# A selective scan in units of 1024 columns: where the carry is copied, and when the halves of each sum are issued

## The chip, the core and the metric

The kernel runs on one core of a Trainium2 chip. The metric is the time of one execution on the device, in microseconds (us); the number compared is the median over runs. In the profile PE is TensorE (PEld its weight loads), DVE is VectorE, ACT is ScalarE, POOL is GpSimd, and SP is SyncE, which issues all of this kernel's DMAs.

## The reference

Two vision blocks follow each other on 8 images of 64x64 tokens with 192 channels. The first is a Mamba-2 block with a depthwise convolution, two scan directions and an MLP. The second splits the channels: 96 go through three convolutions, 96 through a selective scan. The change lies in the selective scan of the second block:

```python
# four directions k: rows, columns, and both reversed; 192 channels d, 16 states n, 4096 tokens l
def step(h, t):
    u_t, d_t, b_t, c_t = t
    h = jnp.exp(d_t[..., None] * A) * h + (d_t * u_t)[..., None] * b_t[:, :, None, :]
    return (h, jnp.einsum('bkdn,bkn->bkd', h, c_t))
...
_, ys = lax.scan(step, h0, scan_in)
ys = jnp.moveaxis(ys, 0, -1) + Ds[None, :, :, None] * xs4
```

So for each direction, channel and state there is a recurrence h[l] = a[l] h[l-1] + b[l] along the tokens, and each output is a sum over the 16 states of h[l] times C[l].

## The kernel before, in words

**Units.** The scan is cut into units. A unit is 128 partitions (8 channels x 16 states) by 1024 tokens (LC). 16 units make a tile of 128 channels, three tiles make a step (the channels of two directions), and each image takes 4 steps forward and 4 steps of the reversed directions: 8 images x 8 steps x 3 tiles x 16 = 3072 units. The unit with the same channels and the next 1024 tokens comes one step, 48 units, later; what it needs is the last column of h of this unit, its carry, kept in the tile `carry`, one column per unit of a step.

**What a unit does.** `fetch(q)` brings in the step sizes, repeated over the states, six units ahead (SP, tile dA, seven buffers). `decay(q)` takes their exponential on ACT two units ahead (L1450). `spread(q)` lets PE repeat the inputs over the states into PSUM, one unit ahead (L1458, tile dB, two buffers). `weigh(q)` multiplies dB by B on DVE (L1473). `scan(q)` runs the recurrence on DVE into h (L1480, seven buffers) and then has POOL multiply h in place by C (L1482), on all columns but the last, which the next step needs unmultiplied. One unit later `carry_on(q)` has ACT copy that column to `carry` (L1488) and then multiply it by C in place (L1489).

**Sums over states.** For four units together `gather` has PE sum the products over the states, with a matrix of zeros and ones: four units go to four groups of 32 partitions of one PSUM tile, 512 columns at a time (L1500, tile acc). After each half ACT copies the PSUM tile to y (L1505, two buffers of y). `store` writes y to DRAM in four DMAs (L1513).

**The order.** All instructions are pinned: each engine runs its own in the order of the program, and so do SP's DMA issues. The main loop goes over q. At the start of a unit come fetch(q+6), weigh(q), and, when due, the making of a gather and a store. Then come two halves. In each half one piece of the gather under way is issued (`next(gathering, None)`), then a piece of other work, then a piece of the preparation of the next tile. The first half ends with carry_on(q-1), spread(q+1) and scan(q), the second with decay(q+2). A gather for units q-5 to q-2 begins in the units q with (q - 2) % 4 == 3. Its first half's matmuls are issued in that unit's first half; the copy of them and the second half's matmuls in its second half; the second copy in the next unit's first half. The store comes at the start of the unit after.

**Work beside.** While the scan of one image runs, `beside` issues everything else: the first block of the next image (conv0, ssd, mlp0), the convolution branch, the scan's inputs, and sums and outputs of earlier images. It has a budget of PE time for each half unit, and a gather's half takes 1.6 us from it (`beside.spend`). All these pieces take their PSUM tiles from one pool of four banks (`cx.one`), the sums over states too.

Of the kernel before, what the change touches and what calls it, by code (L numbers as in the profile page):

```python
# [9 lines left out]
F32 = mybir.dt.float32  # L10
BF16 = mybir.dt.bfloat16
AF = mybir.ActivationFunctionType
# [5 lines left out]
L = HH * WW  # L18
# [20 lines left out]
LC = 1024  # L39
# [1272 lines left out]
def selective_scan(cx, us, ys, beside, images, start_image, tail):  # L1312
# [8 lines left out]
    nc, tc, pin, k = cx.nc, cx.tc, cx.pin, cx.k  # L1321
    AHEAD, BEHIND = 6, 2
    halves = [slice(q * 512, (q + 1) * 512) for q in range(LC // 512)]
    steps = []
# [6 lines left out]
    U = len(units)  # L1331
    per_image = U // images

    def order(ap, g):
        return reversed_free(ap) if g == 1 else ap
# [8 lines left out]
    with (  # L1344
# [6 lines left out]
        u_of, rows_of, bc_of, delta_of, du_of, carries = {}, {}, {}, {}, {}, {}  # L1351
        dAs, dBs, hs, late = {}, {}, {}, []

        def load(m, t):
            image, g, s = steps[m]
            u = wp.tile([128, LC], F32, tag=f"u{t}", name=f"u{t}")
            pin(nc.sync.dma_start(out=u, in_=us(image)[t][:, s * LC : (s + 1) * LC]))
            u_of.setdefault(m, []).append(u)

        def project(m):  # L1360

            image, g, s = steps[m]
            if s == (0, L // LC - 1)[g]:
                carries[image, g] = cp.tile([128, 3, UN], F32, tag="carry", name="carry")
                pin(nc.gpsimd.memset(carries[image, g], 0.0))
            rows = wp.tile([NXP, LC], F32, tag="rows", name="rows")
            for here in halves:
                ps = cx.one("ps_xp")
                for t in range(3):
                    pin(nc.tensor.matmul(  # L1370
                        ps[:NXP], lhsT=k["xp"][:, g, t, :], rhs=u_of[m][t][:, here], start=t == 0, stop=t == 2
                    ))
                    beside.spend(1.2)
                    yield
                pin(nc.scalar.copy(rows[:, here], ps[:NXP]))
            yield
            yield
            bcd = dp.tile([4 * NS, LC], F32, tag="bcd", name="bcd")
            pin(nc.sync.dma_start(out=bcd, in_=rows[0 : 4 * NS]))
            rows_of[m] = rows, bcd  # L1380

        def lay(m, e, i):

            t = wp.tile([128, LC], F32, tag=f"bc{i}{e}", name=f"bc{i}{e}")
            at = NS * (2 * i + e)
            pin(nc.sync.dma_start(out=t, in_=repeated(rows_of[m][1][at : at + NS], True)))
            bc_of.setdefault((m, e), []).append(t)
# [54 lines left out]
        def fetch(q):  # L1442
            n, i = units[q]
            dAs[q] = np_.tile([128, LC], F32, tag="dA", name="dA", bufs=AHEAD + 1)
            pin(nc.sync.dma_start(out=dAs[q], in_=repeated(delta_of[n][UD * i : UD * (i + 1)], False)))

        def decay(q):
            n, i = units[q]
            m, t = tiles[n]
            pin(nc.scalar.activation(dAs[q], dAs[q], AF.Exp, scale=k["neg_a"][:, steps[m][1], t, i : i + 1]))  # L1450

        def spread(q):

            n, i = units[q]
            dBs[q] = pw.tile([128, 2, 512], F32, tag="w", name="dB")
            for half in range(2):
                at = 32 * (2 * (i % 2) + half)
                pin(nc.tensor.matmul(  # L1458
                    dBs[q][:, half, :], lhsT=k["spread"][at : at + 3 * UD, :], rhs=du_of[n][at : at + 3 * UD, i // 2, :],
                    start=True, stop=True,  # L1460
                ))

        def of(q):

            n, i = units[q]
            m, t = tiles[n]
            image, g, _ = steps[m]
            return *bc_of[m, (i // 8 if t == 2 else t)], carries[image, g][:, t, i : i + 1], 0 if g == 1 else LC - 1, g

        def weigh(q):  # L1470

            dBs[q] = dBs[q].rearrange("p a b -> p (a b)")
            pin(nc.vector.tensor_mul(dBs[q], dBs[q], of(q)[0]))  # L1473

        def scan(q):

            _, C_, carry, last, g = of(q)
            dA, dB = dAs.pop(q), dBs.pop(q)
            h = hs[q] = np_.tile([128, LC], F32, tag="h", name="h", bufs=4 + BEHIND + 1)
            pin(nc.vector.tensor_tensor_scan(order(h, g), order(dA, g), order(dB, g), carry, ALU.mult, ALU.add))  # L1480
            rest = slice(1, LC) if last == 0 else slice(0, LC - 1)
            pin(nc.gpsimd.tensor_mul(h[:, rest], h[:, rest], C_[:, rest]))  # L1482

        def carry_on(q):

            _, C_, carry, last, _ = of(q)
            end = hs[q][:, last : last + 1]
            pin(nc.scalar.copy(carry, end))  # L1488
            pin(nc.scalar.activation(end, end, AF.Identity, scale=C_[:, last : last + 1]))  # L1489

        def gather(q):

            n, i = units[q]
            m, t = tiles[n]
            image, g, s = steps[m]
            y = np_.tile([128, LC], F32, tag="y", name="y")
            for here in halves:
                ps = cx.one("acc")
                for v in range(4):
                    pin(nc.tensor.matmul(  # L1500
                        ps[32 * v : 32 * (v + 1)], lhsT=k["gather"], rhs=hs[q - 3 + v][:, here], start=True, stop=True
                    ))
                beside.spend(1.6)
                yield
                pin(nc.scalar.copy(y[:, here], ps))  # L1505
            for v in range(4):
                del hs[q - 3 + v]
            late.append((ys(image)[g][t][UD * (i - 3) : UD * (i + 1), s * LC : (s + 1) * LC], y))

        def store():  # L1510
            rows, y = late.pop()
            for v in range(4):
                pin(nc.sync.dma_start(out=rows[UD * v : UD * (v + 1)], in_=y[32 * v : 32 * v + UD]))  # L1513
# [16 lines left out]
        for q in range(U + BEHIND):  # L1530
            n, at = divmod(q, UN)
            if q < U:
                m, t = tiles[n]
                if q == 0 or q == U - per_image + 2 * BEHIND:
                    start_image(q // per_image, 2 * (per_image - 24))
                if at == 0:
                    coming, due = prepare(n + 1) if n + 1 < len(tiles) else None, 0
                if at in (4, 5):
                    if t == 0:
                        lay(m, 1, at - 4)  # L1540
                    if t == 1 and m + 1 < len(steps):
                        lay(m + 1, 0, at - 4)
                if t == 2 and m + 1 < len(steps):
                    image = steps[m + 1][0]
                    new = image != steps[m][0]
                    if new and at == UN - 8:
                        beside.finish()
                    if UN - 8 <= at < UN - 5:
                        load(m + 1, at - UN + 8)
                    if new and at == UN - 6 and image + 1 < images:  # L1550
                        start_image(image, 2 * per_image)
                    if at == UN - 6:
                        following = project(m + 1)
                if q + AHEAD < U:
                    fetch(q + AHEAD)
                weigh(q)
            elif q == U:
                carry_on(q - 1)
            if (q - BEHIND) % 4 == 3 and q > BEHIND:
                gathering = gather(q - BEHIND)  # L1560
            if (q - BEHIND) % 4 == 1 and q > BEHIND + 1:
                store()
            if q < U:
                for half in range(2):
                    next(gathering, None)
                    beside.half()
                    if coming is not None and 2 * at + half == due:
                        due = next(coming, 2 * UN)
                    if following is not None and t == 2 and at >= UN - 5:
                        next(following, None)  # L1570
                    if half == 0:
                        if q > 0:
                            carry_on(q - 1)
                        if q + 1 < U:
                            spread(q + 1)
                        scan(q)
                    elif q + 2 < U:
                        decay(q + 2)
# [160 lines left out]
```

## Time and profile before

| what | value |
|---|---|
| median of 3 runs | 16,441.98 us (16,431.81 to 16,492.6) |
| span of the profiled execution | 16,436.7 us |
| granted TensorE clock, mean | 0.827 |
| DMA | 3241 MB, 197 GB/s, the hardware queue's packets take 78.5% of 16 engines' span |
| decay, L1450 | 3072 x 1144 ns on ACT |
| sum over states, L1500 | 12,288 passes, 617 ns each in the median |

The profiled execution is one run of its own, and its span goes from the first to the last instruction; it lies 5 us below the median of the runs. A group of instructions is told by line, engine and operation, what it writes and reads, how often it runs, its busy time and the mean of one; behind the second bar stands the time that the engine was idle just before it and what ended most of that. A wait is told as who waited, for whom, the total, how often, and the longest.

### The profile page before, as it was taken

What the parts mean: (1) busy time and instruction counts of PE and PEld (TensorE: products, weight loads), DVE (VectorE), ACT (ScalarE), POOL (GpSimd) and SP (SyncE); (2) the same over time, 40 slices, a digit from 0 to 9 for tenths busy, and PEclk for the clock granted to TensorE, in tenths of its full rate; (3) what the DMA queues carried; (4) which work ended last, traced back from release to release, by engine and by line L of the source; (5) the groups of instructions that cost most, each with busy time, mean ns of one, the idle gap of its engine ahead of it and who ended that gap; (6) DMA issues with size and microseconds to landing.
All of it is one profiled execution on the core that took longest, in us unless ns stands there. A gap on an engine that the chain in (4) does not pass through costs nothing.

```text
span 16436.7 us, 210821 instructions
## 1 busy us (share of the span) xinstructions
PE 13372.1 (81%) x69608; PEld 4636.5 (28%) x69608; DVE 12230.0 (74%) x9264; ACT 10412.7 (63%) x20023; POOL 10527.5 (64%) x5766
## 2 busy tenths in 40 slices
PE   8977887788877897878888788777898788878876
PEld 4423322332223321333223332233322333211111
DVE  2178887886878767887678876788767886778994
ACT  4466677665775757757576575766657666655654
POOL 3158766775668656686567765677656775566773
PEclk9987888789887897878888798887988779877766
DMA  3288888788887888878888778887778877888885
GB/s 89 84 218 195 210 205 225 190 204 208 204 219 187 205 205 207 209 191 204 208 208 207 198 196 198 217 205 197 204 193 221 198 202 205 193 227 200 211 204 137
DMA packets 1602582, 3241.31 MB, mean 197 GB/s; under 512 B 390152, under 2 KB 841368, under 8 KB 1601496
## 3 DMA queue, kind: packets, MB, share of 16 engines
q1 hardware_dynamic: 1601496, 3227.83, 78.5%
q8 instruction: 559, 9.16, 0.3%
q14 instruction: 527, 4.32, 0.1%
HBM read 2548.91 MB, written 678.18 MB: 196 GB/s over the span
## 4 chain that ended last, share of the span: by engine, by line
PE 30%; DMA 16%; DVE 14%; ACT 13%; POOL 7%; issue 5%; SPq 2%; DVEq 0%; ACTq 0%; POOLq 0%
DVE h L1480 9%; DMA dA<-dld 5%; PE acc L1500 5%; DVE dB L1473 4%; PE ps_c L895 4%; PE ps_cv L343 3%; POOL h L1482 3%; ACT dA L1450 3%; PE dB L1458 2%; DMA dus<-dud 2%; PE ps_sum L1193 1%; ACT L107 1%; PE ps_m L799 1%; PE ps_y L696 1%; ACT h L830 1%
## 5 line engine op out<-in xcount | busy, mean ns | idle before, releaser
L1482 POOL TENSOR_TENSOR h<-h,bc 128x1023 f32<-128x1023 f32 x3072 | 7228.8, 2354 | 4585.2 <-DVE h L1480 3895.8
L1480 DVE TENSOR_TENSOR_SCAN h<-dA,carry,dB 128x1024 f32<-128x1024 f32 x3072 | 7200.8, 2344 | 820.7 <-ACT dA L1450 257.6
L1473 DVE TENSOR_TENSOR dB<-dB,bc 128x1024 f32<-128x1024 f32 x3072 | 3736.3, 1216 | 1827.5 <-PE dB L1458 1823.9
L1450 ACT ACTIVATE dA<-dA,neg_a 128x1024 f32<-128x1024 f32 x3072 | 3512.9, 1144 | 29.3 <-DMA dA<-dld 24.1
L1500 PE MATMUL acc<-h,gather 128*32 128x512 f32 x12288 | 2364.1, 730 | 596.5 <-ACT h L1489 329.0
L1458 PE MATMUL dB<-dus,spread 24*128 24x512 bf16 x6144 | 1370.2, 435 | 664.5 <-DVE h L1480 620.1
L1505 ACT COPY y<-acc 128x512 f32<-128x512 f32 x1536 | 884.8, 576 | 750.3 <-PE acc L1500 677.4
L895 PE MATMUL ps_c<-p,conv_w 96*96 96x512 f32 x2304 | 1287.7, 685 | 37.9 <-ACT p L915 26.9
L1488 ACT COPY carry<-h 128x1 f32<-128x1 f32 x3072 | 584.2, 190 | 856.9 <-DVE h L1480 854.4
L1458 PEld LDWEIGHTS <-spread 24*128 24x128 bf16 x6144 | 308.0, 93 | 2837.2 <-issue 1395.5
L1489 ACT ACTIVATE h<-h,bc 128x1 f32<-128x1 f32 x3072 | 905.2, 295 | 143.3 <-ACT carry L1488 1.8
L696 PE MATMUL ps_y<-X,M 64*64 64x64 f32 x12288 | 605.6, 270 | 418.6 <-issue 232.7
L624 ACT ACTIVATE M<-ps_d,ln_dt 128x64 f32<-128x64 f32 x3072 | 669.1, 335 | 314.6 <-PE ps_d L630 304.6
L343 PE MATMUL ps_cv<-pad,diag 64*64 64x512 f32 x6912 | 841.0, 605 | 7.1 <-ACT y L1505 5.1
L1500 PEld LDWEIGHTS acc<-h,gather 128*32 128x32 f32 x12288 | 311.2, 117 | 1636.3 <-issue 1040.1
L107 ACT ACT_TABLE_LOAD x577 | 740.3, 1283 | 10.0
L696 PEld LDWEIGHTS ps_y<-X,M 64*64 64x64 f32 x12288 | 548.8, 180 | 606.5 <-issue 275.5
L629 PE MATMUL ps_d<-R,after 128*128 128x384 f32 x1024 | 606.4, 685 | 31.2 <-ACT bc L618 14.6
L895 PEld LDWEIGHTS ps_c<-p,conv_w 96*96 96x96 f32 x2304 | 372.6, 180 | 785.5 <-issue 725.4
L618 ACT COPY bc<-ps_t 64x256 f32<-64x256 f32 x256 | 93.4, 365 | 716.7 <-PE ps_t L613 716.5
L373 PE MATMUL ps_h<-oa,w1a 128*128 128x256 f32 x1536 | 484.0, 438 | 76.6 <-ACT y L1505 32.2
L1370 PE MATMUL ps_xp<-u,xp 128*108 128x512 f32 x768 | 470.0, 699 | 92.5 <-DMA u<-u 76.0
(243 smaller groups left out, 18412.4 us busy)
## 6 DMA issues: line engine op xcount, KB each, us to landing
dA<-dld SPq DMA_DIRECT2D x3072, 512.0 KB
dud<-terms SPq DMA_DIRECT2D x192, 768.0 KB
dus<-dud SPq DMA_DIRECT2D x2304, 64.0 KB
bc<-bcd SPq DMA_DIRECT2D x256, 512.0 KB
y<-yrows SPq DMA_DIRECT2D x256, 384.0 KB
u<-u SPq DMA_DIRECT2D x192, 512.0 KB
dld<-dl SPq DMA_DIRECT2D x192, 512.0 KB
y<-y SPq DMA_DIRECT2D x3072, 32.0 KB
```

The lines of the kernel that those rows point to most:

```text
L107: self.pin(self.nc.scalar.preload_act_table_set("natural_log_exp_and_others"))
L343: pin(nc.tensor.matmul(ps[64 * b : 64 * (b + 1)].rearrange("p (h w) -> p h w", w=WW), lhsT=diag[:, t, :], rhs=pad[64 * i : 64 * (i + 1), b ...
L696: pin(nc.tensor.matmul(psy[d][here, h * HP : (h + 1) * HP], lhsT=M[here, d, h, :], rhs=X[here, d, h, :], start=True, stop=True,))
L895: pin(nc.tensor.matmul(ps.rearrange("p (h w) -> p h w", w=WW), lhsT=w[:, t, :], rhs=pad[:, dy : dy + RB, dx : dx + WW], start=t == 0, stop ...
L1450: pin(nc.scalar.activation(dAs[q], dAs[q], AF.Exp, scale=k["neg_a"][:, steps[m][1], t, i : i + 1]))
L1458: pin(nc.tensor.matmul(dBs[q][:, half, :], lhsT=k["spread"][at : at + 3 * UD, :], rhs=du_of[n][at : at + 3 * UD, i // 2, :], start=True, s ...
L1473: pin(nc.vector.tensor_mul(dBs[q], dBs[q], of(q)[0]))
L1480: pin(nc.vector.tensor_tensor_scan(order(h, g), order(dA, g), order(dB, g), carry, ALU.mult, ALU.add))
L1482: pin(nc.gpsimd.tensor_mul(h[:, rest], h[:, rest], C_[:, rest]))
L1489: pin(nc.scalar.activation(end, end, AF.Identity, scale=C_[:, last : last + 1]))
L1500: pin(nc.tensor.matmul(ps[32 * v : 32 * (v + 1)], lhsT=k["gather"], rhs=hs[q - 3 + v][:, here], start=True, stop=True))
L1505: pin(nc.scalar.copy(y[:, here], ps))
```

## The change

The carry's copy moves from ACT to POOL, right behind the scan and ahead of POOL's product, which then goes over all 1024 columns in place. It is left out for the last step of an image and direction, whose carry nobody reads. ACT's two instructions of `carry_on` go. In `gather` three empty pieces (`yield`) are put ahead of the second half's matmuls, so that they are issued three half units later than before, in the first half of the unit after next, and the second copy in that unit's second half. The store moves by one unit. h has eight buffers instead of seven and y one instead of two.

```diff
 def of(q):
...
-            image, g, _ = steps[m]
-            return *bc_of[m, (i // 8 if t == 2 else t)], carries[image, g][:, t, i : i + 1], 0 if g == 1 else LC - 1, g
+            image, g, s = steps[m]
+            more = s != (L // LC - 1, 0)[g]
+            bc = bc_of[m, (i // 8 if t == 2 else t)]
+            return *bc, carries[image, g][:, t, i : i + 1], 0 if g == 1 else LC - 1, g, more
...
-            h = hs[q] = np_.tile([128, LC], F32, tag="h", name="h", bufs=4 + BEHIND + 1)
+            h = hs[q] = np_.tile([128, LC], F32, tag="h", name="h", bufs=4 + BEHIND + 2)
             pin(nc.vector.tensor_tensor_scan(order(h, g), order(dA, g), order(dB, g), carry, ALU.mult, ALU.add))
-            rest = slice(1, LC) if last == 0 else slice(0, LC - 1)
-            pin(nc.gpsimd.tensor_mul(h[:, rest], h[:, rest], C_[:, rest]))
-
-        def carry_on(q):
-
-            _, C_, carry, last, _ = of(q)
-            end = hs[q][:, last : last + 1]
-            pin(nc.scalar.copy(carry, end))
-            pin(nc.scalar.activation(end, end, AF.Identity, scale=C_[:, last : last + 1]))
+            if more:
+                pin(nc.gpsimd.tensor_copy(carry, h[:, last : last + 1]))
+            pin(nc.gpsimd.tensor_mul(h, h, C_))
...
-            y = np_.tile([128, LC], F32, tag="y", name="y")
+            y = np_.tile([128, LC], F32, tag="y", name="y", bufs=1)
             for here in halves:
+                if here is halves[1]:
+                    yield
+                    yield
+                    yield
                 ps = cx.one("acc")
...
-            elif q == U:
-                carry_on(q - 1)
             if (q - BEHIND) % 4 == 3 and q > BEHIND:
                 gathering = gather(q - BEHIND)
-            if (q - BEHIND) % 4 == 1 and q > BEHIND + 1:
+            if (q - BEHIND) % 4 == 2 and q > BEHIND + 2:
                 store()
...
                     if half == 0:
-                        if q > 0:
-                            carry_on(q - 1)
                         if q + 1 < U:
                             spread(q + 1)
                         scan(q)
```

More of the change, by code (lines that the diff above doesn't have):

```diff
@@ L1475, in scan @@
         def scan(q):
-            _, C_, carry, last, g = of(q)
+            _, C_, carry, last, g, more = of(q)
             dA, dB = dAs.pop(q), dBs.pop(q)
-            h = hs[q] = np_.tile([128, LC], F32, tag="h", name="h", bufs=4 + BEHIND + 1)
+            h = hs[q] = np_.tile([128, LC], F32, tag="h", name="h", bufs=4 + BEHIND + 2)
             pin(nc.vector.tensor_tensor_scan(order(h, g), order(dA, g), order(dB, g), carry, ALU.mult, ALU.add))
-            rest = slice(1, LC) if last == 0 else slice(0, LC - 1)
-            pin(nc.gpsimd.tensor_mul(h[:, rest], h[:, rest], C_[:, rest]))
-        def carry_on(q):
-            _, C_, carry, last, _ = of(q)
-            end = hs[q][:, last : last + 1]
-            pin(nc.scalar.copy(carry, end))
-            pin(nc.scalar.activation(end, end, AF.Identity, scale=C_[:, last : last + 1]))
+            if more:
+                pin(nc.gpsimd.tensor_copy(carry, h[:, last : last + 1]))
+            pin(nc.gpsimd.tensor_mul(h, h, C_))
         def gather(q):
```

## The prediction

> **What bounds the kernel now.** I read the page first: the busy times, then the chain that ended last.
>
> ```profile
> PE 13372.1 (81%) x69608; PEld 4636.5 (28%) x69608; DVE 12230.0 (74%) x9264; ACT 10412.7 (63%) x20023; POOL 10527.5 (64%) x5766
> PE 30%; DMA 16%; DVE 14%; ACT 13%; POOL 7%; issue 5%; SPq 2%; DVEq 0%; ACTq 0%; POOLq 0%
> ```
>
> No engine is full, and no engine holds more than a third of the chain. 3072 units in 15,290 us (first scan to last) make 4.98 us a unit. DVE needs 2344 + 1216 = 3560 ns of that for the scan and the product into dB; PE, with all that runs beside, needs about 4.3. The two hold each other through the two dB buffers: spread(q+1) waits for scan(q-1), weigh(q+1) waits for spread(q+1). So what counts is not who is busiest but who comes late at a hand-over. That is in the list of waits and in the costliest groups:
>
> ```profile
> L1482 POOL TENSOR_TENSOR h<-h,bc 128x1023 f32<-128x1023 f32 x3072 | 7228.8, 2354 | 4585.2 <-DVE h L1480 3895.8
> L1505 ACT COPY y<-acc 128x512 f32<-128x512 f32 x1536 | 884.8, 576 | 750.3 <-PE acc L1500 677.4
> L1488 ACT COPY carry<-h 128x1 f32<-128x1 f32 x3072 | 584.2, 190 | 856.9 <-DVE h L1480 854.4
> L1489 ACT ACTIVATE h<-h,bc 128x1 f32<-128x1 f32 x3072 | 905.2, 295 | 143.3 <-ACT carry L1488 1.8
> ```
>
> ```profile
> DVE dB L1473 <- PE dB L1458: 1823.9, 718, 99.4
> ...
> ACT carry L1488 <- DVE h L1480: 854.4, 526, 10.1
> ...
> PE acc L1500 <- ACT h L1489: 329.0, 96, 15.9
> PEld acc L1500 <- POOL h L1482: 307.3, 196, 5.4
> ...
> DVE h L1480 <- ACT dA L1450: 257.6, 77, 14.4
> ...
> DVE h L1480 <- ACT carry L1488: 231.4, 90, 9.9
> ```
>
> The columns are total us, times, longest. The reader is to see that ACT's two one-column instructions cost 1489 us of busy time and stop ACT, which works in order, for 854 us behind a scan, and that PE's sums over states stand 329 us for the second of them. The two last rows are one thing: in the records of those waits decay(q) ends 90 ns before the scan, and the carry of unit q-2 merely runs right behind it. So the scan stood 489 us, 167 times, for late decays.
>
> **The change, part by part.** The sum is made against the profiled span, 16,436.7 us; the median of the runs, 16,442, lies 5 above.
>
> (1) The sum over states no longer waits for ACT. It needed the later of POOL's product and ACT's last column; by the records ACT's column ends 0.7 us after the product in the median unit, 6.9 us after in one of ten. PE's waits inside the first halves that ended on h are 133, 368 us together. Were the product alone, 0.3 us later, to release them, 304 us would go. What arrives at the end? The sum stands in PE's order ahead of the next unit's spread, and DVE's idle time before weigh is 945 ns in the unit behind a sum's start against 478 on average in the other three: 0.467 x 768 = 359 us, which holds the wait and the sum's own matmuls. Bounds 0 and -304; I take half, **-150**.
>
> (2) Decays come earlier. Ahead of each decay ACT loses 190 + 295 ns and, per unit, 854/3072 = 0.28 us of standing: 0.76 us. 167 late decays x 0.76 = 127 if one unit's relief arrives; all 489 at most, 0 at least (table loads and activations of the side work are the rest of the lateness). I take **-130**. Other PSUM evictions gain too; not counted.
>
> (3) POOL gets 2304 copies of 128x1 (three of four steps hand a carry on). No such row exists. Nearest:
>
> ```profile
> L418 POOL COPY pad<-pad 128x132 f32<-128x132 f32 x72 | 20.9, 295 | 117.1 <-PE ps_cv L343 117.1
> ...
> L932 POOL COPY p<-p 96x64 f32<-96x64 f32 x56 | 13.2, 235 | 0.0
> ```
>
> ```profile
> L1365 POOL MEMSET carry<- x16: 127/144/153, 791.1 to 15387.1; 128x48 f32 x16
> ```
>
> From 132 to 64 columns the copy loses 60 ns, so at one column about 180; bounds 127 and 235. That is 415 us of POOL (290 to 540). POOL idles 3896 us waiting for scans, which hides most; without that cover all 415 would show. It shows where POOL is the path: 522 us of the chain are this product, 222 instructions, x 0.75 x 0.18 = 30; and beside the layer-0 state recurrence (646 units of 5.83 us by the records, POOL idle 20%) up to 646 x 0.135 = 87. I take **+50**. The product over 1024 columns instead of 1023 adds 2.3 ns x 3072 = 7 us of POOL, at nothing. The copy waits for the scan as the product did, with only the product and POOL's side work queued behind; the carry's reader comes 48 units later, so no scan waits.
>
> Product and scan share no time visibly: the product takes 2326 to 2390 ns and the scan 2325 to 2350 over all 3072, however they overlap, so the copy adds nothing to DVE.
>
> (4) One buffer of y. The first copy of the next sum (half 1 of unit Q+4) must now wait until the four stores of the last (issued at the start of Q+3) have landed. By the completions in the trace (a DMA's landing is the last update of its semaphore before that semaphore's next issue) the last of four stores lands 4.3 us after the first issue in the fastest twentieth, 6.1 in the median, over 10.1 in one of ten. Shifting each landing by one unit and comparing it with the copy's start as it is now: median 0.7 us to spare, but 43% lack time, 1099 us in all. With the issue as early as SP can (0.7 us behind the scan) it is 29% and 515 us. Behind the copy on ACT stand the evictions of the side work and decay(Q+6). What takes the sting out: the lacking cases lie where DVE is nearly full (four units take 18.0 us, DVE idle 1.8; in the others 21.3 and 4.5), a decay ends 4.6 us before its scan in the median, ACT is idle 37%, and (1) and (2) give ACT back 0.76 x 4 = 3.1 us per sum against 1.4 taken. Bounds 0 and +1099; I take a tenth, **+100**.
>
> [...]
>
> (5) Halves apart, eight buffers of h. The second half moves from half 1 of unit Q to the start of Q+2: eight of PE's passes (1.07 us at the full clock) and one 576 ns copy. PE does not wait there, its h being long done. scan(Q+3) takes a buffer read by it, but weigh(Q+3) already stands behind spread(Q+3), which PE issues after it: no new wait. Gain: half the sum's load leaves unit Q+1; at most what (1) leaves of 359, 209. Loss: weigh(Q+3) comes behind 1.07 us more PE work, at worst 768 x the same 0.467 = 359 again. I take **-40**.
>
> [...] The row: the granted clock is 0.827 on average, and a matmul of the sums takes 617 ns in the median but 730 on average. [...]
>
> (6) SP. The stores (four issues of 287 ns) keep their number and go behind the next unit's fetch, half a unit behind the second copy instead of a whole one. That distance is 2.8 us in the median now, so SP will often stand for ACT, 1 to 2 us, with later fetches and the side work's loads queued behind. A dA lands 16 us (5%: 6.4) before its decay starts: **0**; loads of the side work that are closer are in the range.
>
> Sum: -150 - 130 + 50 + 100 - 40 = -170; 16,267, so with the 5 us **16,270 us**.
>
> **Rivals.** *Y's single buffer becomes ACT's stop* (slower). Place: the copy at L1505, once per four units. Price: 1099 us of ACT. The gains without it are 270, 0.35 us per sum, so from the point where a quarter of those 1.43 us per sum reaches PE or DVE, it decides. For it: DMA engines are 80 to 90% busy in most slices and landings reach 10 us; PSUM has four single banks, so an ACT that stands soon stops PE. Against: the cover in (4). At 40%: 440 - 270 = +170, 16,610 us.
>
> *The waits change places* (no change). Freed from ACT, the sum waits for POOL (307 us on that row already, each 0.18 later), DVE still waits 1824 us for PE, whose work is the same. Only (2) remains, at 127, and pays for (3) and (4): 16,442 - 127 + 150 = 16,465 us. For it: PE holds the largest share of the chain.
>
> *ACT was the pacer more than its chain share says* (faster still). All of 304 + 489 goes, y costs nothing: 16,437 - 793 + 50 = 15,694, with the 5 us 15,700 us. Against: the page's chain holds ACT at 13% only.
>
> **How the numbers follow.** Forecast 0.42, larger gain 0.08, no change 0.20, slower by y 0.30. About 0.5% (82 us) is what a measurement of this kernel can tell from no change. The forecast's own range is 16,130 to 16,360. For 8 in 10 it reaches from 15,970 (five eighths of the larger gain) to 16,620 (40% of y's price): below lie 0.07, above 0.13.
>
> **What would show it.** Right: ACT's busy time falls by about 1490 us, the row of PE's sum waiting for ACT is gone and that for POOL grows by less, the scan's wait for decays shrinks, POOL's copy is about 180 ns, and ACT's wait for the y stores stays under 600 us with DVE's wait for PE not grown. Wrong: L1505 waits for DMA above 1000 us and PE's waits for ACT's evictions grow; or the sum's waits for POOL reach what ACT's were; or POOL's small copy takes 400 ns and more.

## The result, and the profile after

The changed kernel takes 17,138.1 us (median of 4 runs, 17,084 to 17,164) against 16,441.8 before: ratio 1.0414, 95% interval 1.039 to 1.0438, 4.1% slower. The profiled execution has a span of 17,082.5 us (16,436.7 before) and a mean granted TensorE clock of 0.809 (0.827). The comparison is made with runs of the kernel before on the same chip.

The page of the changed kernel: busy times, then the costliest groups that answer to those shown of before. The line numbers of scan, product and weigh have moved by two or three.

```profile
PE 13538.7 (79%) x69608; PEld 4675.1 (27%) x69608; DVE 12217.6 (72%) x9264; ACT 9194.9 (54%) x13859; POOL 10944.5 (64%) x8070
...
L1485 POOL TENSOR_TENSOR h<-h,bc 128x1024 f32<-128x1024 f32 x3072 | 7237.8, 2356 | 1596.7 <-DVE h L1482 1279.6
L1505 ACT COPY y<-acc 128x512 f32<-128x512 f32 x1536 | 896.3, 584 | 3886.0 <-DMA y<-y 2324.8
L1484 POOL COPY carry<-h 128x1 f32<-128x1 f32 x2304 | 422.8, 184 | 3196.7 <-DVE h L1482 3056.2
```

Its list of waits (total us, times, longest; rows in between are left out):

```profile
ACT y L1505 <- DMA y<-y: 2324.8, 287, 31.9
...
DVE dB L1475 <- PE dB L1458: 2080.4, 819, 101.0
...
DVE h L1482 <- ACT dA L1450: 952.8, 239, 20.5
...
PEld acc L1500 <- POOL h L1485: 373.4, 214, 7.9
...
PE acc L1500 <- POOL h L1485: 110.1, 88, 6.3
```

The two instructions of ACT are gone, and with them PE's row for ACT's last column (329 and 44 us). POOL's copy takes 184 ns. But a row that was small before is now the largest of ACT. In the kernel before, the view of L1505 has:

```profile
its engine sat idle before it (us, times) until:
...
  DMA y<-y: 12.8, 8
```

Now 287 of the 768 sums find y still being stored, for 8.1 us each. The scan's wait for decays, which was to shrink, has grown from 489 us (the two rows of the prediction, 258 and 231) to 953. The prediction had named these signs against itself: L1505 waiting for DMA above 1000 us, and PE waiting longer for ACT. All idle time of PE and its weight loads that ACT ended, taken over all rows, comes to 2838 us, against 2250 before.

One such case, a long one, from the timeline of the changed kernel (start, duration, engine, line, operation, and in brackets the idle time before it and what ended it; SPq is SP's queue of DMA issues; lines in between are left out):

```profile
1026.07 7.22 SPq L1434 DMA_DIRECT2D dus<-dud  x6
1027.16 0.60 ACT L1505 COPY y<-acc 128x512 f32<-128x512 f32 x1
...
1033.94 0.52 SPq L1445 DMA_DIRECT2D dA<-dld  x1
...
1036.40 3.48 SPq L1434 DMA_DIRECT2D dus<-dud  x6
1037.19 0.39 PE L1458 MATMUL dB<-dus,spread 24*128 24x512 bf16 x2
1038.24 2.35 DVE L1482 TENSOR_TENSOR_SCAN h<-dA,carry,dB 128x1024 f32<-128x1024 f32 x1
1040.93 0.52 SPq L1445 DMA_DIRECT2D dA<-dld  x1
1041.55 1.45 SPq L1513 DMA_DIRECT2D y<-y  x4
...
1046.68 0.59 ACT L1505 COPY y<-acc 128x512 f32<-128x512 f32 x1 [12.50 <-DMA y<-y]
1047.16 1.15 ACT L1450 ACTIVATE dA<-dA,neg_a 128x1024 f32<-128x1024 f32 x1
1047.32 4.47 PE L343 MATMUL ps_cv<-pad,diag 64*64 64x512 f32 x16 [9.74 <-ACT y L1505]
1048.40 2.35 DVE L1482 TENSOR_TENSOR_SCAN h<-dA,carry,dB 128x1024 f32<-128x1024 f32 x1 [6.69 <-ACT dA L1450]
...
1054.19 1.23 DVE L1475 TENSOR_TENSOR dB<-dB,bc 128x1024 f32<-128x1024 f32 x1 [3.44 <-PE dB L1458]
```

The second copy of a sum ends at 1027.76. Its stores are issued 13.8 us later: they stand on SP's queue behind two groups of six dus loads, two fetches and two stores of the work beside, and the last fetch waits for the scan that frees its dA, which ends at 1040.59. The next sum's first copy waits until 1046.68. Behind it on ACT, in order, stand the decay that the next scan needs (DVE idle 6.69 us) and the stage's evictions, ACT's copies of the work beside out of PSUM (PE idle 9.74 us); once PE is late, DVE waits for the spread too (3.44 us). This stop is paid on both of the engines that set the pace.

### The profile page after: what moved, and what is told of

Its sections match the earlier page's. It is cut to its first block, busy times and chain, and to the rows that moved or that the text cites. A ratio compares the mean times of both kernels' runs of the same rounds, so it can differ in the third digit from the quotient of the medians.

```text
span 17082.5 us, 207825 instructions
## 1 busy us (share of the span) xinstructions
PE 13538.7 (79%) x69608; PEld 4675.1 (27%) x69608; DVE 12217.6 (72%) x9264; ACT 9194.9 (54%) x13859; POOL 10944.5 (64%) x8070
## 5 line engine op out<-in xcount | busy, mean ns | idle before, releaser
L1485 POOL TENSOR_TENSOR h<-h,bc 128x1024 f32<-128x1024 f32 x3072 | 7237.8, 2356 | 1596.7 <-DVE h L1482 1279.6
L1450 ACT ACTIVATE dA<-dA,neg_a 128x1024 f32<-128x1024 f32 x3072 | 3470.0, 1153 | 27.4 <-DMA dA<-dld 21.6
L1505 ACT COPY y<-acc 128x512 f32<-128x512 f32 x1536 | 896.3, 584 | 3886.0 <-DMA y<-y 2324.8
L1500 PE MATMUL acc<-h,gather 128*32 128x512 f32 x12288 | 2271.5, 739 | 367.9 <-POOL h L1485 110.1
L1484 POOL COPY carry<-h 128x1 f32<-128x1 f32 x2304 | 422.8, 184 | 3196.7 <-DVE h L1482 3056.2
L895 PE MATMUL ps_c<-p,conv_w 96*96 96x512 f32 x2304 | 1239.0, 664 | 67.7 <-ACT p L915 63.1
L343 PE MATMUL ps_cv<-pad,diag 64*64 64x512 f32 x6912 | 872.9, 607 | 28.7 <-ACT y L1505 15.2
L1409 POOL TENSOR_TENSOR du<-dl,u 128x1024 f32<-128x1024 f32 x192 | 452.1, 2355 | 174.4 <-ACT dl L1406 90.6
L599 POOL TENSOR_TENSOR R<-upto,da 128x768 f32<-128x768 f32 x256 | 376.5, 1471 | 182.0 <-PE ps_d L629 167.8
```

The costliest lines, as they stand in the source:

```text
L343: pin(nc.tensor.matmul(ps[64 * b : 64 * (b + 1)].rearrange("p (h w) -> p h w", w=WW), lhsT=diag[:, t, :], rhs=pad[64 * i : 64 * (i + 1), b ...
L895: pin(nc.tensor.matmul(ps.rearrange("p (h w) -> p h w", w=WW), lhsT=w[:, t, :], rhs=pad[:, dy : dy + RB, dx : dx + WW], start=t == 0, stop ...
L1485: pin(nc.gpsimd.tensor_mul(h, h, C_))
L1500: pin(nc.tensor.matmul(ps[32 * v : 32 * (v + 1)], lhsT=k["gather"], rhs=hs[q - 3 + v][:, here], start=True, stop=True))
```

## The experiments

Times are medians; ratios are to the kernel before on the same chip, with the 95% interval. The first eight runs ask which part of the change costs, the next four why, the last six what is left over.

**The carry alone.** The kernel before with the carry on POOL; y, h and the halves as before.

```diff
-            rest = slice(1, LC) if last == 0 else slice(0, LC - 1)
-            pin(nc.gpsimd.tensor_mul(h[:, rest], h[:, rest], C_[:, rest]))
+            if more:
+                pin(nc.gpsimd.tensor_copy(carry, h[:, last : last + 1]))
+            pin(nc.gpsimd.tensor_mul(h, h, C_))
```

> The kernel before with the carry's move alone: POOL copies the carry and multiplies all columns; halves close together, seven buffers of h, two of y. Theory Y (y's single buffer stops ACT, decays come late, DVE stands): no wait of the y copy for stores, the scan's wait for decays at or below the 489 us of before, 16,150 to 16,440 us. Rival P (the copies on POOL delay products and with them the sums): most of the loss is here, 16,800 to 17,100 us, with PE's waits for POOL's product doubled. Rival H (it is the distance of the halves): no loss here, 16,350 to 16,500 us.

Measured: 16,355.7 us, ratio 0.995 [0.9934, 0.9966]. Its list of waits:

```profile
DVE h L1482 <- ACT dA L1450: 447.8, 163, 14.0
...
PEld acc L1496 <- POOL h L1485: 373.2, 226, 5.4
...
PE acc L1496 <- POOL h L1485: 100.8, 96, 4.5
```

The carry's move gains 0.5%, some 80 us, where steps (1) to (3) of the prediction came to 230. The sum's waits for ACT are gone, and those for POOL rise from 371 to 474 us. But the scan's waits for decays, 489 us before with the two rows taken together, are still 448. ACT is relieved, and the median decay ends 5.1 us ahead of its scan instead of 4.7, but the decays that came late still do.

**One y alone.** The kernel before with `bufs=1` for y, and again with one y of double width, so that the other buffers keep their places.

```diff
-            y = np_.tile([128, LC], F32, tag="y", name="y")
+            y = np_.tile([128, LC], F32, tag="y", name="y", bufs=1)
```

> The kernel before with one buffer of y instead of two and nothing else: the store comes one unit and a half after the second copy's issue and two and a half units before the next first copy. Theory Y: the stores have mostly landed, the y copy waits for stores under 400 us in all, 16,430 to 16,600 us; the buffer harms through its distance to the store, which only the halves' move makes short. Rivals P and H: 16,440 us, no change.

> The kernel before with one buffer of y of twice the width, of which the first half is used: one buffer, but every tile lies where it lay before. If the 1.5% of the one buffer alone come from the wait, it is again 16,640 to 16,730 us; if they come from the moved tiles, 16,400 to 16,480 us.

Measured: 16,686.9 us, 1.0154 [1.0137, 1.017], and 16,645.4 us, 1.0127 [1.0106, 1.0148]. The y copies wait only 215 us (77 times) in the first, 200 us in the second. The two don't go together: a loss of 210 to 250 us can hardly come from 200 us of waits on an engine that is idle a third of the time. The second kernel was to tell the wait from moved tiles, and by its expectation it spoke for the wait; that reading was wrong, as the last experiments show.

**Halves apart, without the carry's move**, and **the whole change with two y**. For the room of its second y the second has dA fetched five units ahead instead of six, in one buffer less; a control has that and one y.

```diff
-    AHEAD, BEHIND = 6, 2
+    AHEAD, BEHIND = 5, 2
...
-            y = np_.tile([128, LC], F32, tag="y", name="y", bufs=1)
+            y = np_.tile([128, LC], F32, tag="y", name="y")
```

> The change without the carry's move: halves one and a half units apart, eight buffers of h, one of y, the carry still on ACT. Theory Y: the y copy waits 1000 to 2000 us for stores, 16,900 to 17,200 us. Rival P: nothing lost, about 16,400 us. Rival H: 16,900 to 17,200 us as well, but then without a large wait of the y copy for stores.

> The changed kernel with two buffers of y; to make room dA is fetched five units ahead instead of six. Theory Y: the wait for the stores is gone, the scan's wait for decays falls from 953 us below 500, and the time is back at 16,250 to 16,550 us. Rivals P and H: it stays at 16,950 to 17,200 us, since POOL's copies and the distance of the halves are the same.

> Control for the kernel with two buffers of y: the changed kernel with one buffer of y and dA fetched five units ahead. Theory Y: as the changed kernel, 17,000 to 17,250 us, so that the recovery with two buffers is the buffer's. Rival: fetching nearer clears SP's queue and alone brings 16,400 to 16,700 us.

Measured: 17,253.8 us, 1.0495 [1.0473, 1.0516], for the halves apart with one y and the carry on ACT, where the y copies wait 1834 us; 16,393.2 us, 0.9971 [0.9954, 0.9988], for the change with two y; 17,131.8 us, 1.0423 [1.0403, 1.0444], for the control. The first kernel has no copy on POOL and yet the whole loss, and this row of waits:

```profile
ACT y L1509 <- DMA y<-y: 1833.8, 273, 24.3
```

The second y takes 739 us (17,131.8 less 16,393.2) off the change, and the five units ahead nothing. The same list of waits with two y:

```profile
DVE dB L1475 <- PE dB L1458: 1950.6, 706, 99.8
...
DVE h L1482 <- ACT dA L1450: 445.0, 145, 25.8
```

The row of y waiting for its stores is gone, and the scan's waits for decays are back at 445. Halves apart cost little with two y (16,393 against 16,356), and 567 us with one (17,254 against 16,687): the distance is dear only where y is single. Halves close leave three and a half units between a sum's second copy and the next sum's first; halves apart leave two, and the store stands half a unit behind its copy instead of a whole one.

**Shorter holds.** The changed kernel with y as two tiles of 512 columns, each stored by itself (eight stores of 16 KB for a sum); and with the stores issued from ACT's queue right behind the second copy.

```diff
-                pin(nc.scalar.copy(y[:, here], ps))
+                y = np_.tile([128, 512], F32, tag=f"y{here.start}", name="y", bufs=1)
+                pin(nc.scalar.copy(y, ps))
...
-            if (q - BEHIND) % 4 == 2 and q > BEHIND + 2:
+            if (q - BEHIND) % 4 in (0, 2) and q > BEHIND + 2:
                 store()
```

```diff
-                pin(nc.sync.dma_start(out=rows[UD * v : UD * (v + 1)], in_=y[32 * v : 32 * v + UD]))
+                pin(nc.scalar.dma_start(out=rows[UD * v : UD * (v + 1)], in_=y[32 * v : 32 * v + UD]))
```

> The changed kernel with the one buffer of y cut in two tiles of 512 columns, each stored by itself (first half at the start of unit Q+1, second at Q+3; eight stores of 16 KB a sum instead of four of 32 KB). Same room in SBUF, same order of halves, same carry. Theory Y: each tile has three and a half units from its store's place to its next copy, so the copies wait under 150 us for stores in all, the scan's wait for decays falls to about 450 us, and the time is 16,330 to 16,500 us. Rival L (one more change of layout or the room taken from y, not the wait): it stays at 17,000 us and more.

> The changed kernel, one buffer of y, with the four stores issued from ACT's own queue right behind the second copy instead of from SP behind the next unit's fetch. If the store's place in SP's queue makes the wait (in the waits of the changed kernel the second copy ends 0.9 us before the scan that the fetch waits for, and the first store is issued 5.0 us behind it), the landing comes some 5 us earlier, the copy's waits fall from 2325 to under 700 us and the time to 16,400 to 16,750 us, with some 900 us of issuing on ACT in it. If the landing itself is what is slow, the waits stay above 1500 us and the time at 17,000 us or more.

Measured: 16,674.9 us, 1.0144 [1.0124, 1.0164], with 541 us of y waits; 17,578.6 us, 1.0697 [1.0678, 1.0715], with 170. Freeing each half by itself takes back 463 us, less than expected: the y waits were to fall under 150 us, and 282 us more than the time with two y remain. ACT's queue is the wrong place for the stores. Two of its rows of waits:

```profile
ACT dA L1450 <- DMA y<-y: 571.1, 254, 11.8
...
ACT y L1505 <- DMA y<-y: 170.0, 80, 4.8
```

The y wait is nearly gone and the kernel slower still by 440 us, with DVE's wait for PE at 2698 us (2080 in the changed kernel). ACT's idle time that is put down to these stores is 1315 us over all rows, and the largest row is that of the decays: the wait has changed its name. The four issues take 988 us of ACT's queue in all (306 ns each in the median). The expectation had counted some 900 us of that, but not what stands behind it.

**The stores' place on SP, and the decay's on ACT.** If the hold is SP's queue, the stores ahead of the unit's fetch help. If the stop reaches DVE by the decay behind the copy, the decay ahead of it helps.

```diff
             n, at = divmod(q, UN)
+            if (q - BEHIND) % 4 == 2 and q > BEHIND + 2:
+                store()
             if q < U:
...
                 if q + AHEAD < U:
                     fetch(q + AHEAD)
                 weigh(q)
             if (q - BEHIND) % 4 == 3 and q > BEHIND:
                 gathering = gather(q - BEHIND)
-            if (q - BEHIND) % 4 == 2 and q > BEHIND + 2:
-                store()
```

```diff
                 for half in range(2):
+                    if half == 1 and q + 2 < U:
+                        decay(q + 2)
                     next(gathering, None)
...
-                    elif q + 2 < U:
-                        decay(q + 2)
```

> The changed kernel with the four stores of a sum issued ahead of the unit's fetch instead of behind it; all else as changed. Queue theory (the single buffer of y is held long because its stores stand behind the 512 KB fetch of that unit on SP's queue): in the waited cases the fetch is issued 3.2 us and the first store 5.0 us after the scan that frees them, so the stores go out some 2 us sooner and need not share the DMA engines with the fetch that now follows them; the y copies' 2325 us of waiting fall by 287 x 2 to 3 us, to about 1500 to 1750, and the time, at the same share (745 us for 2325), to about 16,900 to 16,950. Rival (the waiting of SP for the y copy then holds the fetch itself, and the decays come late): waits of the decay for its fetch grow above 300 us and the time stays at 17,140 or goes above it. Second rival (the hold is the transfer itself, not its place in the queue): y waits stay above 2100 us, time within 80 us of 17,140.

> The changed kernel with each unit's decay (the exponential on ACT) put ahead of the work of the second half, and so ahead of the first y copy, instead of behind it. Theory that the wait for the single buffer reaches DVE through the decay queued behind the waiting copy on ACT: the scans' waits for decays fall from 983 us to 300 to 470 (470 is what the kernels without y waits show), the y copies still wait some 2000 to 2500 us, and the time falls by 400 to 500 us to 16,640 to 16,750. Rival (the wait reaches PE and DVE through the stage's own work behind the copy on ACT, the decays only being the first that shows): scans' waits for decays fall as much, DVE's other waits (for ACT's work of the stage, for PE's spread) rise in their place, and the time stays within 120 us of 17,140.

> The changed kernel with both moves: stores ahead of the fetch and decay ahead of the first y copy. If the single buffer's loss is the hold (queue) times what stands behind it on ACT (decays), the two gains add: 16,400 to 16,550 with the one buffer of y kept. If either mechanism is not it, the time is that of the better of the two alone.

Measured: stores first 16,748.9 us, 1.0185 [1.0161, 1.0209]; decay first 16,995.6, 1.034 [1.0322, 1.0359]; both 16,715.7, 1.0176 [1.0155, 1.0198]. SP's own waits in the changed kernel, and then in the kernel with the stores first:

```profile
SPq L1445 <- DVE h L1482: 4267.2, 1665, 11.0
SPq L1513 <- ACT y L1505: 400.4, 160, 13.4
```

```profile
SPq L1445 <- DVE h L1482: 3034.6, 1260, 9.5
SPq L1513 <- ACT y L1505: 1455.7, 412, 12.0
```

The place on SP is about half of the loss: 389 us come back, and the y copies wait 1354.5 us (188 times), 970 less. What SP stands is nearly the same and only in another place: 1233 us less for the scans ahead of its fetches, 1055 more for ACT ahead of the stores. The gain is larger than the queue theory gave (190 to 240). It lies where that theory puts it: over the four units from each waiting copy of the changed kernel on, those 287 sums take 367 us less in all, and the others 28 us more.

The list of waits with the decay first:

```profile
DVE dB L1475 <- PE dB L1458: 2591.5, 864, 101.4
ACT y L1505 <- DMA y<-y: 2210.7, 283, 30.5
...
DVE h L1482 <- ACT dA L1450: 367.8, 83, 16.4
```

The scan's wait for decays falls by 585 us, and DVE's wait for PE's spread rises by 511 in its place: 143 us come back, a little more than the rival's bound of 120, far from the 400 to 500 of the theory. The decay was only the first thing behind the copy. Behind it stand the stage's evictions, and PE with them: the idle time of PE and its weight loads that ACT ended stays at 2908 us (2838 in the changed kernel, 1979 with two y). With the stores first as well it adds just 33 us, so the two gains don't add.

**The decay first, without the changed y and halves**: the kernel with the carry alone, and the edit just shown.

> The kernel before with the carry on POOL alone (16,356 us) and the decay put ahead of the work of the second half. If the decays' place is worth something without a late y: the scans' waits for decays, 471 us there, fall to some 200 and the time to 16,100 to 16,250. Rival (the stage's work on ACT, now behind the decay, is as urgent): the time stays within 80 us of 16,356 or goes above it.

Measured: 16,198.9 us (16,156 to 16,228), 0.9855 [0.983, 0.9879]: the fastest version, 1.45% ahead of the kernel before and 5.5% ahead of the changed one. Its waits:

```profile
DVE dB L1475 <- PE dB L1458: 1752.5, 697, 104.1
...
DVE h L1482 <- ACT dA L1450: 250.2, 64, 15.6
```

Here the scan's waits for decays do shrink (448 to 250), and DVE's wait for PE does not rise in their place (1751 with the carry alone). The copy of a sum has little part in this. With the carry alone only the decay of one unit in four stands behind the copy that the edit moves it past, and by the records that decay has 18 of the 163 late cases and 51 of the 448 us. The rest stood behind the other work of the half unit: the pieces beside and the preparation of the next tile. In the changed kernel, where the copy waits for y, the same decay has 643 of the 953 us.

**What one y alone had cost.** The tiles that the stages and the sums take from the pool of four PSUM banks get their banks when the program is built. With one y, on the same program in the same order, 1035 of the 1536 tiles of acc and 572 of the 896 of ps_h (the layer-0 state recurrence) lie in another bank than before, so other pairs of tiles wait for each other. The kernel with the y of double width has the very banks of the one-y build, which is why it could not tell the two apart. Four kernels cross the two: each tile's bank is written into the kernel, as the build of another version chose it.

```diff
-        self.singles.append(self.singles.pop(0))
-        return self.singles[-1].tile([128, 512], F32, tag="n", name=name)
+        return self.banks[next(self.at)].tile([128, 512], F32, tag="n", name=name)
...
-    cx.singles = [ctx.enter_context(tc.tile_pool(name="ps", bufs=4, space=PSUM))]
+    for i in range(4):
+        cx.banks[str(i)] = ctx.enter_context(tc.tile_pool(name=f"ps{i}", bufs=1, space=PSUM))
```

> The kernel before with one buffer of y, each PSUM tile put by hand into the bank that it has in the kernel before. If the 1.5% of the single y there are the banks: 16,440 to 16,500 (what is left is the part of 215 us of waits that reaches the end, a third). If they are the wait for y: 16,640 to 16,700 as with the banks that the build chose.

> The kernel before with its two buffers of y, each PSUM tile put by hand into the bank that it has in the version with one y. If the banks are the loss: 16,580 to 16,690, with the layer-0 state recurrence at some 6.05 us a unit. If the wait for y is: 16,400 to 16,470 and 5.83 us a unit there.

> The changed kernel (one y) with each PSUM tile in the bank that it has in the version with two y. If the wait for y is the loss of the change: within 120 us of 17,138, y waits of 2000 us and more. If the banks are a main part of it: 16,700 to 16,950 with y waits as long as before.

> The changed kernel with two buffers of y (dA fetched five units ahead to make room) and each PSUM tile in the bank that it has in the changed kernel. If the wait for y is the loss: within 100 us of 16,393. If the banks are a main part: 16,600 to 16,850.

| program | two y | one y |
|---|---|---|
| before, banks of before | 16,437 | 16,482: 1.0021 [1.0007, 1.0034] |
| before, banks of the one-y build | 16,670: 1.0129 [1.011, 1.0148] | 16,687: 1.0154 [1.0137, 1.017] |
| change, banks of its two-y build | 16,393: 0.9971 [0.9954, 0.9988] | 17,165: 1.0437 [1.042, 1.0454] |
| change, banks of its own build | 16,584: 1.0084 [1.0064, 1.0104] | 17,138: 1.0414 [1.039, 1.0438] |

(All two-y versions of the change have dA five units ahead; the control with one y and five ahead has the same banks as the changed kernel.) For the kernel before the answer is plain: of the 1.5% with one y the banks are 1.3% and the wait 0.2%. The list of waits of the kernel with two y and the other banks has the row that tells it; in the kernel before that wait comes to 9 us:

```profile
PE ps_h L763 <- DVE Hn L769: 158.0, 72, 3.6
```

The state recurrence takes 6.06 us a unit there, and 5.83 with the banks of before, with one y or two. For the change itself the wait is the main loss: one y costs 772 us in the one set of banks and 554 in the other, and the banks alone 191 us with two y and nothing with one (17,165 against 17,138). The kernel with two y in the other banks fell between its two expectations (within 100 us of 16,393, or 16,600 and above). The two don't add; that the waits for banks hide where ACT stands for y would explain it, but no run shows it. The banks were not held in the experiments on shorter holds and on the places of stores and decay, where most tiles of acc lie elsewhere than in the changed kernel; what they gained can hold a part of that size, up to 191 us.

The same was asked of the versions with the carry on POOL, in the banks of the kernel before.

> The kernel before with the carry on POOL alone, each PSUM tile in the bank of the kernel before. If the 61 us lost in the layer-0 state recurrence are POOL's copies: within 40 us of 16,356. If they are the banks: 16,260 to 16,310.

> Carry on POOL and decay ahead of the second half's work, each PSUM tile in the bank of the kernel before. If that order's gain of 157 us is its own: within 60 us of 16,199. If part of it was a better choice of banks: 16,270 and above.

Measured: 16,348.0 us, 0.9945 [0.9927, 0.9963], and 16,216.8 us, 0.9866 [0.9841, 0.9891]. Within 20 us of the builds' own choice: POOL's price in the state recurrence (5.91 us a unit, 5.83 before) and the order's gain are their own.

## Why the prediction was wrong

It said 16,270 us, and the time is 17,138. The forecast had y's single buffer as one small term; the rival that made it ACT's stop had the right place and the right sign, and gave 16,610 (the four single banks that it names are those of the kernel's pool). By the prediction's own sum 88% of the 1099 us, not 40%, would have had to count to give the time measured; in truth the waits were twice as long, and a smaller share of them counted.

**Step (4), the single y: failed.** Taken at +100 with bounds of 0 and +1099, it measured +554 to +772 us. Two things in it were wrong, and they multiply.

The first is how long y is held. I shifted each landing of before by one unit: 43% of the sums lack time, 1099 us, 3.3 us each. The share was right (287 of 768 is 37%), the size was not: 8.1 us each. Even the better case had the stores leave 0.7 us behind the scan. In the waited cases of the changed kernel, by the records, the fetch is issued 3.4 us behind the scan's end (median), the first store at 5.3, and the last has landed at 13.3. A shifted trace keeps the queue of before; behind the fetch the stores inherit all that the fetch waits for. That is more than the scan: where the fetch is over 1 us late (186 of the 287 cases), the issue just ahead of it is a dus load in 148. Step (6) asked only what the stores would delay, which is little, and not what would delay the stores, which is about half of the loss (stores first: 389 of 745 us).

Both parts of the hold are longer in the waited cases than in the others. From the second copy's end to the first issue it is 5.6 us in the median against 1.1, and from the first issue to the last landing 7.3 against 4.8 (5.4 over all). For the second part the prediction took 6.1 us, the median in the trace of before, and the larger part of what it missed lies ahead of the issue.

The second is what a stop of ACT costs. I took a tenth of it, since the lacking sums lie where DVE is nearly full. That argument runs the wrong way. Where DVE is full, four units pass quickly, which is why time lacks there, and a stop of DVE finds no slack. For the 287 waited sums the four units from the waiting copy's on took 18.9 us together in the version with two y and 21.7 in the changed kernel: 784 us more over all of them. The same units of the other sums took 78 us less in all. Among the 287, the third in which DVE had under 0.2 us of idle time in these units with two y lost 0.44 us for each us of wait, and the third in which it had over 2.9 us lost 0.20. ACT's 37% idle time was no cover either, because the wait stands in the middle of an ordered queue: 2325 us of waits turned into a quarter to a third of that.

**Steps (1) to (3), the carry's move: right in sign, a third of the size.** -230 was taken, -80 measured. The sum's waits for ACT went (373 us), those for POOL grew by 103, the copy takes 184 ns against 180 taken. Step (2) was the most mis-sized: the scan's waits for decays, taken at -130, fell by 41 us in the kernel with the carry alone. The 0.76 us of relief priced for each decay reached the median one as 0.4, and the late ones hardly. I priced an engine's load; what set the late decays was the order, the other work of the half unit ahead of them. Put ahead of that work they gave 157 us. Step (3) came near its +50: with the banks held, POOL's copies cost 0.08 us in each of 646 units of the state recurrence, 52 us. Of step (1)'s 150 that would leave some 90, an estimate from these three numbers (80 + 52 - 41); no run measures it by itself. ACT's busy time fell by 1218 us, not 1490: busy time counts overlapping instructions once, and on ACT they overlap a little (the copy at 1046.68 ends after the decay at 1047.16 has begun), by 1238 us in all before and 985 after.

**Step (5), halves apart: small, as taken, but its sign isn't shown.** -40 was taken, and with two y it measured +38 (16,393 against 16,356), less than a measurement tells from nothing, and in other banks. The matmuls of the sums hardly pay for being less close together: one takes 739 ns in the mean with the halves apart and two y, 737 with the carry alone. But the step was priced by itself: it also takes one and a half units from the time that y has, and without that one y costs 0.2%.

## What to carry to other kernels

When a buffer is taken away and something else moves in the same change, price them together: the time between the last reader and the next writer has to hold the wait for the queue position of the release (here 5.6 us in the waited cases), not just the transfer (7.3 us). A stop in an in-order engine is dearest where the bound engine is full, since there no slack takes it (0.44 us lost for each us of wait, against 0.20 where DVE had idle time). And relief of an engine does little for an instruction that is late by its place in the order (the scan's waits for decays fell by 41 us with ACT relieved, and by 198 more with the decays moved): move the instruction.

## What the runs showed of the hardware

**TensorE's granted clock was 0.5 behind stops of PE.** In the records of the kernel before and of the changed one it is 1.0 or 0.5, for whole numbers of steps of 3.41 us. The windows around the case shown above, in the changed kernel (busy us and instructions of PE, PEld, DVE, ACT and POOL, granted clock, DMA share, GB/s):

```profile
1033.90:1037.60 3.70, 3.68 (x16) 0.76 (x15) 3.57 (x3) 0.28 (x1) 2.64 (x3) 1.00 0.86 192
1037.60:1041.00 3.40, 0.00 (x0) 0.00 (x0) 3.27 (x3) 0.00 (x0) 2.32 (x3) 1.00 0.81 258
1041.00:1044.40 3.40, 0.00 (x0) 0.00 (x0) 0.71 (x1) 0.00 (x0) 2.26 (x1) 0.50 0.78 208
1044.40:1047.80 3.40, 0.48 (x2) 0.29 (x4) 0.00 (x0) 1.12 (x2) 0.00 (x0) 0.50 1.00 249
1047.80:1051.20 3.40, 3.40 (x16) 0.99 (x12) 2.35 (x1) 2.39 (x5) 0.31 (x2) 0.50 1.05 269
1051.20:1054.60 3.40, 3.40 (x30) 0.73 (x30) 0.41 (x1) 1.66 (x3) 2.23 (x1) 0.99 0.99 293
```

The second window has no matmuls, and in the next three the clock is 0.50; in the last of these PE is busy throughout, and behind it the clock is back at 0.99. The 16 matmuls of L343 behind the stop take 4.47 us, nearly all of it at 0.50; eight of the same shape, at 1052.71 us, take 1.09. Over the changed kernel's 561 falls PE was busy for 40% of the 3.41 us ahead of the fall in the median; ahead of a rise it was busy for all of them, in the median too. PE has 600 gaps above 2 us there and 503 in the version with two y, the time at half clock is 6513 against 6037 us, and PE's busy time for the same matmuls 13,539 against 13,377. That is some 160 us more of PE; how much of it reaches the end no run shows.

**The choice of PSUM banks was worth 1%.** The same instructions in the same order differ by 1.3% (before) and 1.1% (the change with two y) with nothing but the bank of each tile in a pool of four. An edit to an SBUF buffer moved them (1035 of the 1536 tiles of acc), so an experiment of this case that changes a count of buffers measures this too unless the banks are held.
